# Two attention layers on one core: v's weights loaded twice, and another order for loads, combinations and the first layer 1 projections

## Chip, core and metric

The kernel runs on one core of one Trainium2 chip. The metric is the device time of one execution in microseconds (us). The median of three runs of the kernel before is 4241.31 us (4237.41 to 4242.2). Engines are called PE (matrix multiply), DVE (vector), ACT (scalar and activation functions), POOL and SP; SP only issues transfers here, and ACT and POOL can issue them too.

## What is computed

The input x is 8 images of 512 channels and 1024 tokens (32 x 32). All is float32. In short:

```python
def gn(v):                      # per image and group of 16 channels (G=32)
    return (v - mean) / sqrt(var + eps)

def layer0(x):                  # 8 heads of 64 channels
    n = gn(x) * gn_w + gn_b
    q, k, v = split(qkv_w @ n + qkv_b)
    a = softmax((q*s)^T (k*s)) @ v
    return proj_w @ (x + a) + proj_b

def layer1(x):
    q, k, v = w_q @ x, w_k @ x, w_v @ x
    attn = einsum('gh,bhqT->bgqT', w_head, q^T k * scale)   # heads are mixed
    attn = softmax(attn)
    attn = (attn - mean) / sqrt(var + eps) * gamma + beta   # per image and head
    return w_proj @ rearranged(attn @ v) + b_proj

x = x + layer0(gn(x))
x = x + layer1(gn(x))
```

## The kernel before

One program runs everything. Batches (images) are taken one after the other: layer 0 for all eight, with its result kept in DRAM (`x1_d`), then layer 1 for all eight. Within each engine the instructions run in the order in which the Python code issues them, apart from a short setup of constants ahead of that. Work that must be slipped between other work is put into an `Agenda`: `ag.at(slot, fn)` stores a function, and `ag.run(slot)` calls what is stored for that slot, in the order in which it was stored.

**Projections.** A projection of 512 x 512 weights with a 512 x 1024 right side is done with seven half-size products instead of eight. The weights' side needs seven tiles: three are blocks loaded as they are, four are sums and differences. `load_blocks(which)` (lines 747 to 763) issues eight DMAs of 128 KB; `combine_left(which)` (lines 765 to 776) makes the four combinations on DVE (parts 0 to 3) and stores all seven tiles to DRAM (part 4, on SP), from where `load_left` fetches them in later batches. The tag `left` has two buffers, so a third set waits until the first is free. The right side's combinations are `combine_right` (lines 882 to 885). `project0` runs the seven products on PE: products 1 and 2, then 6, 5, 7, 3 and 4, with ACT or DVE taking each out of PSUM (the addition of product 6 is line 932, that of product 7 line 939). Products 1 and 4 use the two PSUM buffers `a0`, products 5 to 7 the two double tiles `s`.

**Start of the kernel.** SP issues the four loads of x for batch 0. `load_blocks("k", nc.scalar)` and the same for v issue theirs from ACT. POOL loads the small vectors, qkv's bias among them and, last, `whT`. DVE copies the bias into `bq`, takes x's statistics (`bn_stats`, line 648), and with a small matmul (`pm`, line 622) the group means follow. A tiny matmul `pw` (line 555) belongs to the setup. Then come, in the code's order: `combine_right`, `combine_left("k")`, `qk0(0,"k")`, `combine_left("v")`, `load_blocks("q")`, `combine_left("q")`, `v0(0)`, `load_blocks("p")`, `combine_left("p")`, `qk0(0,"q")`, and attention of batch 0.

**Seam.** In the last batch of layer 0, `first_k1`, `first_q1` and `first_v1` project k, q and half of v of layer 1's batch 0. q's copy is written in another order of elements, with strided views (line 1019). The final totals of the attention (matmul `z`, line 1128, in an `a0` buffer) fall between the two projections. `out0` follows.

**Layer 1.** A batch has NX = 32 half steps, numbered x, and some after them. Half step x does the scores of x (line 1656, PE), copies them to a tile `raw` (ACT and DVE), and does for older steps: mixing of heads (`mix` of y = x - 4, line 1706), exponentials, sums and squares, and `values` (line 1752). Two half steps make one t. Before mixing, the tile `raw` of t is regrouped by eight DMAs of 256 KB each (`regroup`, line 1682, index r) into one half of `re_t`; t takes the half (t + b) % 2. In the first half steps (x up to 4) all eight are issued at once; later they are tied one by one to matmuls.

v is made in four pairs of 128-token blocks (`v_pair`, line 1475): pairs 0 and 1 between the steps that close the batch before, pairs 2 and 3 among the first scores. v's weights (`load_w`, line 1339, four DMAs of 256 KB) lie in that half of `re_t` which t = 1 will fill, in its first four r. So pairs 2 and 3 must be done before the regroups r = 0 to 3 of t = 1 may be issued: the code gives t = 1 its own order, and puts pair 3 into slot 3 - 0.75, which half step 3 runs ahead of its regroups. In batch 0 the group statistics of batch 7 (`group_stages`: means, squares, root) and `v_sums` fall here too. A PSUM tile of the tag `m` (three buffers) is held until its last reader has been issued and is done; scores, mixes, pairs and the small matmuls of the statistics all use this tag.

The sums of exponentials are kept in a tile `z` (tag `z`, one buffer, 1 MB) and their squares in `z2`; a quarter of the batch (`qb`) uses them from its first `squares` to its `totals`.

Between two batches the order is: k's projection of the next batch among the last half steps, pair 0, the division and the affine step, the output projection `out1` with its loads `xs` and the load of left_q, pair 1, q's projection.

Of the kernel before, what the change touches and what calls it, by code (L numbers as in the profile page):

```python
# [9 lines left out]
F32 = mybir.dt.float32  # L10
# [8 lines left out]
P = 128  # L19
# [448 lines left out]
def tile_two_attention_layers(  # L468
# [19 lines left out]
    nc = tc.nc  # L488
    B, C, T = x_d.shape
    H = w_head.shape[0]  # L490
    D = C // H
    NCC = C // P
# [28 lines left out]
    qkvb = column("qkvb", qkv_b)  # L521
# [175 lines left out]
    with ExitStack() as l0:  # L697
# [49 lines left out]
        def load_blocks(which, queue=nc.sync, tag="u0"):  # L747

            t = left_tile(which, 0)
            if tag == "junk":  # L750
                a21[which] = zpool.tile([P, T], F32, tag=tag, name=f"a21_{which}", bufs=1)[
                    :, :C
                ].rearrange("p (k o) -> p k o", k=2)
            else:
                a21[which] = zpool.tile([P, 2, HC], F32, tag=tag, name=f"a21_{which}")
            for dst, i, j in (
                (t[:, 0], 0, 0), (t[:, 1], 0, 1), (a21[which], 1, 0), (t[:, 2], 1, 1),
            ):
                for k in range(2):
                    queue.dma_start(  # L760
                        out=dst[:, k],
                        in_=SOURCES[which][ts(2 * j + k, P), i * HC : (i + 1) * HC],
                    )
# [11 lines left out]
            if 4 in parts:  # L775
                nc.sync.dma_start(out=left_d[which], in_=t.rearrange("p f k o -> p (f k o)"))

        load_blocks("k", nc.scalar)
        load_blocks("v", nc.scalar)


        bq = wpool.tile([P, 3, NCC], F32, tag="bq", name="bq", bufs=1)
        nc.vector.tensor_copy(bq.rearrange("p i c -> p (i c)"), qkvb)

        st0 = {}
        n_t, xa_t, q_t, k_t, v_t = {}, {}, {}, {}, {}
# [404 lines left out]
        qk0(0, "k")  # L1191
        combine_left("v")
        load_blocks("q")
        combine_left("q")
        v0(0)
        load_blocks("p")
        combine_left("p")
        qk0(0, "q")
        tmp.clear()

        for b in range(B):
            more = b + 1 < B
            ag = Agenda()
            ag.at(1, lambda: bias_xa(b))
            for c in range(NCC):
                ag.at(2 + 2 * c, lambda c=c: start_xa(b, c))
            for c, slot in enumerate((4, 7, 12, 15)):
                if b > 0:
                    ag.at(slot, lambda c=c: stats_out(b - 1, c))
                if more:  # L1210
                    ag.at(slot + 1, lambda c=c: load_x(b + 1, c))
            if b < 3:

                which = ("k1", "q1", "p1")[b]
                ag.at(1, lambda which=which: load_blocks(which, tag="junk"))
                for i, slot in enumerate((13, 14, 16, 17, 19)):
                    ag.at(slot, lambda which=which, i=i: combine_left(which, [i]))
            if more:
                stats0(b + 1, ag, 20)
                for c in range(NCC):  # L1220
                    ag.at(49 + 4 * c, lambda c=c: normalize0(b + 1, c))
                ag.at(32, lambda: load_left("k", b + 1))
                ag.at(33, lambda: load_left("v", b + 1))
            else:

                def load_first():
                    t = n_t["1"] = shared.tile([P, NCC, T], F32, tag="n", name="y_0")
                    for c in range(NCC):
                        nc.sync.dma_start(out=t[:, c], in_=x1_d[0][ts(c, P), :])

                ag.at(20, load_first)
                for slot, fn in zip((22, 25, 28), group_stages(0, B - 1, small_psum)):
                    ag.at(slot, fn)
                ag.at(32, lambda: load_left("k1", 0))
                ag.at(33, lambda: load_left("q1", 0))
                for c in range(NCC):
                    ag.at(49 + 4 * c, lambda c=c: normalize_to(n_t["1"][:, c], 0, c))
            attention0(b, ag)
            slot = NI + 2
            if more:  # L1240
                combine_right(f"{b + 1}", n_t[b + 1])
                qk0(b + 1, "k")
            else:
                combine_right("y1", n_t["1"])
                first_k1()
            ag.flush()
            if more:
                load_left("q", b + 1)
                v0(b + 1)
                load_left("p", b)  # L1250
                qk0(b + 1, "q")
            else:
                load_left("p", b)
                first_q1()
                first_wv()
            combine_right(f"{b}_xa", xa_t[b])
            out0(b)
            tmp.clear()
# [6 lines left out]
    with ExitStack() as l1:  # L1265
# [373 lines left out]
        class Attention1:  # L1639
# [5 lines left out]
            def scores(self, x, i):  # L1645

                b, t, hp = self.b, x // 2, x % 2 * 2 + i
                qb, kb = t // NKB, t % NKB
                nm = f"s1_{b}_{x}_{i}"
                ps = m_psum(nm)  # L1650
                pv = ps.rearrange("p m (j k) -> p m j k", j=2)
                for j in range(2):
                    for c in range(2):
                        for m in range(2):
                            r = slice(m * D, m * D + D)
                            last = nc.tensor.matmul(  # L1656
                                pv[c * D : c * D + D, m, j],
                                qo_t[b][r, 2 * qb + j, hp, ts(c, D)],
                                k_t[b][r, hp, ts(kb, KB)], start=True, stop=True,
                            )  # L1660
                if x > MLAG:
                    self.piece(last)
                if x % 2 and i == 1:

                    order = (4, 5, 6, 7, 0, 1, 2, 3) if t == 1 else R_ORDER
                    self.due = [(t, r) for r in order]
                if x % 2 == 0 and i == 0:
                    self.raw[t] = rawpool.tile([P, H, 2, KB], F32, tag="raw", name=f"raw_{b}_{t}")
                dst = self.raw[t][:, 2 * hp : 2 * hp + 2]
                if i == (x == 0) and (x < MLAG or x % 2):  # L1670
                    nc.vector.tensor_copy(dst, pv)  # L1671
                else:
                    nc.scalar.copy(dst, pv)  # L1673
# [205 lines left out]
            def half_step(self, x, ag):  # L1879
                y, w = x - MLAG, x - MLAG - 1  # L1880
                if 0 <= w < NX:
                    self.squares(w, 0)
                    self.sum_e(w, 0)
                if x < NX:
                    self.scores(x, 0)
                if 0 <= w < NX:
                    self.squares(w, 1)
                    self.sum_e(w, 1)
                if x < NX + MLAG:
                    k_leave()  # L1890
                if 0 <= w < NX:
                    self.sum_e2(w, 0)
                    self.sum_e2(w, 1)
                k_leave()
                if 0 <= y < NX:
                    self.mix(y, 0)
                if 0 <= w < NX:
                    self.values(w, 0)
                if x < NX:
                    self.scores(x, 1)  # L1900
                if 0 <= y < NX:
                    self.mix(y, 1)
                ag.run(x - 0.75)
                if x <= MLAG or x >= NX:
                    self.regroup(n=NR)
                if x >= NX:
                    self.piece(n=len(self.pieces))
                ag.run(x - 0.5)
                if 0 <= w < NX:
                    self.values(w, 1)  # L1910
                    self.e.pop(w)
                    if w % QLAG == QLAG - 1:
                        qb = w // QLAG
                        self.leave(qb)
                        self.totals(qb)
                        if qb < NQB - 1:
                            ag.at(x + 2, lambda: self.reciprocals(qb, ag, x + 2))
                            ag.at(x + 6, lambda: self.divide(qb))
                ag.run(x)


        load_w(("v", 0), wvT, re_t[:, 1, : NCC * C])

        NV = NT // 4
        for b in range(B):
            more = b + 1 < B
            a = Attention1(b)
            ag = Agenda()

            for i, slot in enumerate((1, 3 - 0.75)):  # L1930
                ag.at(slot, lambda i=i: v_pair(b, NV + i))
            if b == 0:
                for x, fn in enumerate(group_stages(B - 1, B, small_psum1)):
                    ag.at(x, fn)
                ag.at(3 - 0.75, v_sums)
            free = (NX // 2 - 2 + b) % 2
            if more:
                a.pieces += [lambda i=i: y_piece(b + 1, i) for i in range(4 * NCC)]
# [43 lines left out]
            op = out1(b, right_o)  # L1982
            load_left(("q", b + 1))
            v_pair(b + 1, 1)
            op.run()
            q_projection(b + 1).run()

# [69 lines left out]
```

## Time and profile before

| | |
|---|---|
| median of three runs | 4241.31 us |
| the profiled execution's own time | 4225.8 us |
| its span, first to last instruction | 4223.7 us |
| first k matmul of layer 0 | 24.16 us |
| first scores of layer 0 | 104.38 us |
| first scores of layer 1, batch 0 | 1813.03 us |
| first mix of layer 1, batch 0 | 1847.57 us |
| a group of first scores in batches 1 to 7 of layer 1 | 2132.39, 2439.50, 2745.39, 3052.20, 3357.86, 3662.68, 3967.83 us |
| DMA, all queues | 521.99 MB, mean 124 GB/s |

The page shows one profiled execution. Groups of instructions are named by line, engine, operation and tiles; a timeline row gives start, duration, engine, line, operation, what is written and read, and in brackets how long the engine had stood before and who released it. "issue" in the place of a releaser means that the engine waited for nothing that the profile shows. The profiled execution is 15.5 us shorter than the median of the timed runs; its parts are compared with each other and with those of another profiled execution.

The costliest groups of each engine, for scale (idle time of the engine ahead of them after the bar):

```profile
L1706 PE MATMUL m<-wmix,re 64*64 64x64 f32 x32768 | 591.2, 219 | 17.3 <-issue 12.0
L1752 PE MATMUL a<-e,v 128*64 128x256 f32 x4096 | 556.3, 392 | 2.6 <-ACT z L1723 1.7
L1656 PE MATMUL s<-k,q 64*64 64x256 f32 x8192 | 553.7, 388 | 5.6 <-DVE q L1512 2.6
```

### The profile page before, as it was taken

How to read it: one execution, taken by the hardware profiler on the slowest of the kernel's cores; microseconds unless marked ns; L12 is line 12 of the kernel's file. 1: busy time of each engine (PE TensorE's matmuls, PEld its weight loads, DVE VectorE, ACT ScalarE, POOL GpSimd, SP SyncE). 2: the span in 40 equal slices, each digit the busy share in tenths (PEclk: the TensorE clock that was granted, in tenths of full speed). 3: DMA queues.
4: the chain of work that ended last, by engine and by line, in shares of the span. 5: the costliest groups of instructions: out<-in, count | busy, mean ns of one | idle time of the engine just before them, and what ended most of it. 6: DMA issues, size and time to landing. Idle time of an engine off the chain costs nothing.

```text
span 4223.7 us, 131372 instructions
## 1 busy us (share of the span) xinstructions
PE 4147.2 (98%) x58572; PEld 2212.8 (52%) x58572; DVE 2861.1 (68%) x3780; ACT 2317.5 (55%) x2735; POOL 60.3 (1%) x86
## 2 busy tenths in 40 slices
PE   7999999999999999999999999999999999999998
PEld 4353535353535353356556466466466466466565
DVE  4748484747475757558758668668578578588587
ACT  1717272726263635358358368278287187286386
POOL 0000000000000000000000000000000000000000
PEclk9999999999999999999999999999999999999999
DMA  4213131212121212167467367277287386385475
GB/s 150 79 45 114 46 111 48 84 48 84 46 86 43 87 45 86 43 156 196 141 149 194 125 172 193 104 192 186 104 204 188 95 205 168 112 207 150 135 183 141
DMA packets 253871, 521.99 MB, mean 124 GB/s; under 512 B 51888, under 2 KB 59440, under 8 KB 246640
## 3 DMA queue, kind: packets, MB, share of 16 engines
q1 hardware_dynamic: 248416, 510.71, 42.6%
q8 instruction: 461, 7.55, 0.7%
q0 software_dynamic: 2576, 0.69, 0.4%
q10 hardware_dynamic: 2304, 2.10, 0.2%
q14 instruction: 114, 0.93, 0.1%
HBM read 197.16 MB, written 46.92 MB: 58 GB/s over the span
## 4 chain that ended last, share of the span: by engine, by line
PE 92%; DVE 4%; DMA 2%; ACT 1%; issue 1%; SPq 0%; POOL 0%; DVEq 0%; ACTq 0%; POOLq 0%
PE a L1752 12%; PE s L1656 11%; PE m L1706 11%; PE s L1083 11%; PE a L1109 10%; PE pp_p L903 5%; PE pk_p L903 5%; PE pq_p L903 4%; PE pv_p L903 4%; PE pk L1400 4%; PE pq L1400 4%; PE pv L1475 4%; PE pp L1400 3%; PE t L1783 1%; DMA re<-raw 1%
## 5 line engine op out<-in xcount | busy, mean ns | idle before, releaser
L1706 PEld LDWEIGHTS m<-wmix,re 64*64 64x64 f32 x32768 | 580.5, 135 | 113.3 <-issue 49.1
L1088 ACT ACTIVATE e<-s 128x1024 f32<-128x1024 f32 x512 | 497.2, 1026 | 233.6 <-PE s L1083 232.6
L1706 PE MATMUL m<-wmix,re 64*64 64x64 f32 x32768 | 591.2, 219 | 17.3 <-issue 12.0
L1712 ACT ACTIVATE e<-m 128x1024 f32<-128x1024 f32 x512 | 526.2, 1028 | 135.7 <-PE m L1706 132.1
L1730 DVE TENSOR_TENSOR z<-z,e 128x1024 f32<-128x1024 f32 x448 | 537.9, 1220 | 72.2 <-ACT e L1712 72.0
L1734 DVE TENSOR_TENSOR z<-z,e 128x1024 f32<-128x1024 f32 x448 | 534.7, 1221 | 61.9 <-ACT e L1723 60.8
L1656 PE MATMUL s<-k,q 64*64 64x256 f32 x8192 | 553.7, 388 | 5.6 <-DVE q L1512 2.6
L1752 PE MATMUL a<-e,v 128*64 128x256 f32 x4096 | 556.3, 392 | 2.6 <-ACT z L1723 1.7
L1096 DVE TENSOR_TENSOR zacc<-zacc,e 128x1024 f32<-128x1024 f32 x384 | 468.8, 1221 | 87.0 <-ACT e L1088 65.9
L1673 ACT COPY raw<-s 128x1024 f32<-128x1024 f32 x368 | 372.9, 1013 | 269.2 <-PE s L1656 232.0
L1083 PE MATMUL s<-q,k 64*64 64x512 f32 x4096 | 490.1, 593 | 2.3 <-ACT e L1088 2.3
L1109 PE MATMUL a<-e,v 64*64 64x512 f32 x4096 | 484.0, 589 | 0.0
L1723 ACT ACTIVATE e<-e 128x1024 f32<-128x1024 f32 x448 | 460.2, 1057 | 0.0
L1656 PEld LDWEIGHTS s<-k,q 64*64 64x64 f32 x8192 | 269.0, 132 | 269.2 <-issue 164.4
L1752 PEld LDWEIGHTS a<-e,v 128*64 128x64 f32 x4096 | 250.5, 136 | 123.6 <-issue 13.0
L1109 PEld LDWEIGHTS a<-e,v 64*64 64x64 f32 x4096 | 156.6, 133 | 282.9 <-issue 282.9
L1083 PEld LDWEIGHTS s<-q,k 64*64 64x64 f32 x4096 | 147.8, 133 | 275.3 <-issue 241.4
L1671 DVE COPY raw<-s 128x1024 f32<-128x1024 f32 x144 | 176.0, 1222 | 91.1 <-PE s L1656 84.8
L1475 PE MATMUL pv<-re,y 128*128 128x512 f32 x480 | 214.8, 601 | 0.0
L1475 PEld LDWEIGHTS pv<-re,y 128*128 128x128 f32 x480 | 89.3, 191 | 113.5 <-issue 112.7
L903 PE MATMUL pv_p<-left_v,tmp 128*128 128x256 f32 x512 | 114.9, 383 | 4.2 <-DVE tmp L932 4.2
L1480 DVE COPY v<-pv 128x512 f32<-128x512 f32 x30 | 20.7, 690 | 138.4 <-ACT v L1479 138.4
(315 smaller groups left out, 4051.5 us busy)
## 6 DMA issues: line engine op xcount, KB each, us to landing
re<-raw SPq DMA_DIRECT2D x1024, 256.0 KB
rzb<-zd SPq DMA_DIRECT2D x256, 128.0 KB
left_q<-left_q SPq DMA_DIRECT2D x17, 1792.0 KB
left_p<-left_p SPq DMA_DIRECT2D x17, 1792.0 KB
left_k<-left_k SPq DMA_DIRECT2D x10, 1792.0 KB
x<-in_x_dram SPq DMA_DIRECT2D x32, 512.0 KB
x<-x SPq DMA_DIRECT2D x64, 256.0 KB
left_v<-left_v SPq DMA_DIRECT2D x8, 1792.0 KB
```

The costliest lines, as they stand in the source:

```text
L903: nc.tensor.matmul(out, st, mv, start=start, stop=(k == 1), skip_group_check=True)
L1083: nc.tensor.matmul(ps[c * D : c * D + D, m], k[r, hp, k0 : k0 + D], q[r, hp, ts(f, FB)], start=True, stop=True,)
L1088: nc.scalar.activation(e[i], ps, AF.Exp, scale=S0 * S0)
L1096: nc.vector.tensor_add(zacc[g], zacc[g], e[i])
L1109: nc.tensor.matmul(acc[g][a][m * D : m * D + D], v[rows, kc, ts(2 * hp + m, D)], e[i][rows, m], start=(kc == 0), stop=(kc == NG - 1),)
L1475: nc.tensor.matmul(ps[:, m], y_t[b][:, c, ts(2 * i + m, P)], w[:, c], start=(c == 0), stop=(c == NCC - 1),)
L1656: last = nc.tensor.matmul(pv[c * D : c * D + D, m, j], qo_t[b][r, 2 * qb + j, hp, ts(c, D)], k_t[b][r, hp, ts(kb, KB)], start=True, stop=True,
L1706: last = nc.tensor.matmul(ps[c * D : c * D + D, a, ts(r, D)], self.re[t, r][rows, j, k0 : k0 + D], wmix[rows].rearrange("p g i -> p (g i)" ...
L1712: nc.scalar.activation(self.e[y][:, j], ps.rearrange("p a c -> p (a c)"), AF.Exp)
L1730: nc.vector.tensor_add(self.z[:, j], self.z[:, j], self.e[y][:, j])
L1734: nc.vector.tensor_add(self.z2[:, j], self.z2[:, j], self.e2[j])
L1752: last = nc.tensor.matmul(self.acc[w][two * D : two * D + D, s].rearrange("p (c i) -> p c i", i=Q8), v_t[b][:, kc, ts(g, D)], e[:, g], sta ...
```

## The change

The diff does these things:

1. `load_blocks("k")` and `load_blocks("v")` are issued from SP, in the code's order behind x's four loads. `bq` is a view of `qkvb` instead of a copy.
2. `combine_left("q")` moves behind `v0(0)`, its store behind `qk0(0,"q")`; `combine_left("p")` moves behind `qk0(0,"q")` and q's store.
3. `first_q1` comes before `first_k1`, and their loads change places too.
4. In layer 1, a new function `load_wv_again(b)` loads v's weights into a tile of the tag `z`. It is called ahead of batch 0, in place of the load into `re_t`, and for each later batch after pair 1, so that pairs 2 and 3 (and `v_sums`) read that tile. The load into `re_t` near the end of each batch stays for pairs 0 and 1.
5. t = 1 is regrouped in the same order as every t. Pair 3 and `v_sums` move from slot 3 - 0.75 to slot 3, the call for slots x - 0.75 is gone, and the group statistics' three stages are put into slots 0, 1 and 3 ahead of the pairs (before: 0, 1 and 2, behind the pair in slot 1).

```diff
-        load_blocks("k", nc.scalar)
-        load_blocks("v", nc.scalar)
-
-
-        bq = wpool.tile([P, 3, NCC], F32, tag="bq", name="bq", bufs=1)
-        nc.vector.tensor_copy(bq.rearrange("p i c -> p (i c)"), qkvb)
+        load_blocks("k")
+        load_blocks("v")
+
+
+        bq = qkvb.rearrange("p (i c) -> p i c", i=3)
...
         load_blocks("q")
-        combine_left("q")
         v0(0)
+        combine_left("q", range(4))
         load_blocks("p")
+        qk0(0, "q")
+        combine_left("q", [4])
         combine_left("p")
-        qk0(0, "q")
         tmp.clear()
...
-                ag.at(32, lambda: load_left("k1", 0))
-                ag.at(33, lambda: load_left("q1", 0))
+                ag.at(32, lambda: load_left("q1", 0))
+                ag.at(33, lambda: load_left("k1", 0))
...
                 combine_right("y1", n_t["1"])
-                first_k1()
+                first_q1()
...
                 load_left("p", b)
-                first_q1()
+                first_k1()
                 first_wv()
...
                 if x % 2 and i == 1:
-
-                    order = (4, 5, 6, 7, 0, 1, 2, 3) if t == 1 else R_ORDER
-                    self.due = [(t, r) for r in order]
+                    self.due = [(t, r) for r in R_ORDER]
...
-                ag.run(x - 0.75)
                 if x <= MLAG or x >= NX:
                     self.regroup(n=NR)
...
-        load_w(("v", 0), wvT, re_t[:, 1, : NCC * C])
+        def load_wv_again(b):
+
+            t = zpool.tile([P, 2, T], F32, tag="z", name=f"wv_{b}")
+            load_w(("v", b), wvT, t.rearrange("p j c -> p (j c)"))
+
+        load_wv_again(0)
...
-            for i, slot in enumerate((1, 3 - 0.75)):
-                ag.at(slot, lambda i=i: v_pair(b, NV + i))
             if b == 0:
-                for x, fn in enumerate(group_stages(B - 1, B, small_psum1)):
+                for x, fn in zip((0, 1, 3), group_stages(B - 1, B, small_psum1)):
                     ag.at(x, fn)
-                ag.at(3 - 0.75, v_sums)
+            for i in range(NV):
+                ag.at(1 + 2 * i, lambda i=i: v_pair(b, NV + i))
+            if b == 0:
+                ag.at(3, v_sums)
...
             v_pair(b + 1, 1)
+            load_wv_again(b + 1)
             op.run()
```

## The prediction

> **What bounds the kernel now.** I read the page first: busy table, slices, chain by line. Then the gaps on PE in order of time through the timeline, then the timeline of all engines around each gap that the diff touches.
>
> ```profile
> PE 4147.2 (98%) x58572; PEld 2212.8 (52%) x58572; DVE 2861.1 (68%) x3780; ACT 2317.5 (55%) x2735; POOL 60.3 (1%) x86
> ...
> PE 92%; DVE 4%; DMA 2%; ACT 1%; issue 1%; SPq 0%; POOL 0%; DVEq 0%; ACTq 0%; POOLq 0%
> ```
>
> PE is busy for 4147.2 of 4223.7 us and holds 92% of the chain. No matmul is added or removed, so all that the change can win or lose is the 76.5 us in which PE stands. The Trainium skill (Perfetto Trace Analysis, "Identifying the Most-Contended Engine") says that matmul busy time is no measure of the distance to the roofline; I use it only to find the gaps. The list of PE's waits over the whole span names those that matter:
>
> ```profile
> PE pw L555 <- DVE eye L551: 17.4, 1, 17.4
> PE m L1706 <- issue: 12.0, 22, 1.4
> ...
> PE pv_p L903 <- DVE tmp L932: 4.2, 1, 4.2
> PE pk_p L903 <- DVE n L861: 4.2, 1, 4.2
> ```
>
> The columns are: who waited for whom, us in total, times, longest. The first and fourth are the start of the kernel, the third is the first v projection, the second is spread over layer 1. The seam between the layers adds rows of 1 to 3 us. Each is taken below.
>
> **The change, part by part.** Everything is summed against the profiled execution (span 4223.7, its own time 4225.8), and the gain is then taken off the median.
>
> **Part 1, start.** k's and v's blocks go from ACT's queue to SP's, behind the four x loads; the copy into bq is gone.
>
> ```profile
> 10.80 0.17 DVE L783 COPY bq<-qkvb 128x12 f32<-128x12 f32 x1 [9.58 <-DMA qkvb<-in_qkv_b_dram]
> ...
> 18.56 0.16 DVE L626 COPY gs_gm<-pm 128x4 f32<-128x4 f32 x1 [0.28 <-PE pm L622]
> ...
> 24.16 8.53 PE L903 MATMUL pk_p<-n,left_k 128*128 128x512 f32 x16 [4.19 <-DVE n L861]
> ```
>
> DVE is in order and stands until 10.80 for the bias of qkv, with the statistics of x queued behind. They then run without a gap for 5.7 us, the last tile's from 15.11. In the packets of the DMA queues x's last one lands near 14.2 us, because k's and v's 2.1 MB share the engines: the skill (DMA: Bandwidth & Descriptors, "Issuing engines are not separate DMA queues", and "Queues, rings and completion order") says that queues issued by different engines run on the same 16 DMA engines, which serve them in turn. The trace agrees: while SP's and ACT's queues are both full the engines move 180 to 390 GB/s for both together. So dropping the copy alone is worth at most 15.11 - 14.2 = 0.9 us. With x alone in front, 2.1 MB at the 333 to 394 GB/s of the stretch from 3 to 6 us, and a start at 1.8, are in by 8 to 9 us, the last statistics end near 10.2 instead of 16.6. What is late next: PE's tiny matmul pw (line 555) stands ahead of the statistics' pm in PE's queue and needs whT, a POOL DMA issued at 6.56 that takes 7.1 us to land, 13.7 us. Then pw 0.59, pm and the copy gs_gm near 14.85 instead of 18.56: 3.7 us. If pm is ordered ahead of pw, or whT lands earlier, up to 16.6 - 10.2 = 6.4. I take 4.0, range 0.9 to 6.4. The k blocks issue from about 6.5 us on SP and are in by 14, before n is ready near 20; v's by 17, needed near 46. Nothing on SP waits behind them but left_k's store, issued at 32.1.
>
> **Part 2, combinations.** q's go behind v0, p's behind q's projection.
>
> ```profile
> 64.47 0.69 DVE L768 TENSOR_TENSOR left_q<-a_q,left_q 128x512 f32<-128x512 f32 x1 [11.30 <-DMA left_q<-in_qkv_wT_dram]
> ...
> 67.01 1.21 DVE L932 TENSOR_TENSOR tmp<-tmp,pv_p 128x1024 f32<-128x1024 f32 x1
> ...
> 68.28 5.23 PE L903 MATMUL pv_p<-left_v,tmp 128*128 128x256 f32 x16 [4.21 <-DVE tmp L932]
> ```
>
> DVE's queue holds q's four combinations ahead of v0's addition at line 932. They wait until 64.47 for q's blocks, which came behind left_v's store; the addition, ready near 60.5 (its product is the first half of PE's 7.07 us from 57.00), runs at 67.01 and PE stands 4.21 us for the PSUM tile that it frees. With the combinations behind v0 the addition runs at once: -4.2, and I find nothing that takes its place. The combinations (4 x 0.69 = 2.7 us) then run while PE does the first 16 matmuls of q (7.0 us), which read only loaded blocks. q's store (SP) now stands behind p's eight issues (3.6 us) and nobody waits for it soon. p's combinations run on DVE after q's last additions, 2.7 us ahead of nb and the first zacc; ACT's first use of nb came at 109.60, 4.3 us after it was made at 105.34, so they fit; without that cover they would cost at most 2.7. I take 0.
>
> **Part 3, q1 before k1.** q1's strided additions take 2.05 us a pair (line 1019), k1's 1.28 (line 1002). PE's 1.72 us stand before out0 is the time until the last of q1's are out of PSUM. Now it falls after q1, where the totals' matmul z (0.57) and its row copy use the same two PSUM tiles: PE resumes about 2.8 us after q1's end, against 0.8 now between k1's end and q1's start; after k1 out0 starts with no stand. Net +0.2, range -0.3 to +1.
>
> **Part 4, start of layer 1, batch 0.** The squares of the group statistics go ahead of the v pair, the root from slot 2 to slot 3.
>
> ```profile
> 1830.52 0.36 PE L633 MATMUL pv<-gs_sq,gavg 128*128 128x4 f32 x2 [2.15 <-DVE gs_sq L631]
> ...
> 1833.25 1.96 PE L1656 MATMUL s<-k,q 64*64 64x256 f32 x32 [0.48 <-DVE raw L1671]
> ```
>
> PE's 2.15 and 0.48 us stands come from a chain of four small DVE operations behind the v pair's copies. Ahead of the pair the chain (four steps of 0.2) starts when raw's copy ends, 1820.06, so PE stands 0.9. But its PSUM tile is then held until slot 3, so the scores of x = 2 and 3 share two tiles of three: I count 0.5 + 0.2 + 0.4 of new stands. 2.63 - 2.0 = -0.6, range -1.8 to +1.5. The first pair's weights, loaded to another tile, arrive before 1820 either way.
>
> **Part 5, the second load of v's weights and the regroups of t = 1.** This is the part that repeats, seven times.
>
> ```profile
> 2442.55 19.15 SPq L1682 DMA_DIRECT2D re<-raw  x16
> ...
> 2464.38 0.27 PE L1706 MATMUL m<-wmix,re 64*64 64x64 f32 x2 [1.43 <-issue]
> ```
>
> Half of t = 1's regroups write where v's weights lie, and wait for the batch's last v pair (7.13 us from 2452.08) to end, 2459.2; the 1 MB then lands by 2464.7, under the first mixes, which issue most instructions per us. At that place PE stands in batches 1 to 7 for 0.76, 1.43, 1.34, 0.76, 1.66, 0.47 and 0.34 us: 6.8 us together. What stands there reads t = 0's rows, landed by 2452, so it isn't their data. I take it for instruction fetch: the skill (Advanced Engine Details and Errata, "ISA Cache") gives blocks of 16 KB, 256 instructions; queue 8's 461 packets of 7.55 MB are such blocks, and one moved in the us from 2461. The stands end as the regroups' packets end. With the weights in the sums' tile all eight regroups go from 2453 and, at t = 0's 8.7 us for 2 MB, end near 2462.5, 2.2 us earlier than now; that clears most. I take -5.0, range 0 to -7. Batch 0 has no stand there, so nothing.
>
> What it adds: four DMAs of 256 KB on SP per batch, after left_q's and before the output's stores. SP waits for nothing there (the sums' tile was last read by the totals at 2067, the issue comes near 2078). The loads end near 2091 where left_q's packets ended at 2088.2; the first pair that reads them starts at 2134, and the tile's first sum comes after both pairs. x's and left_q's transfers are ahead of them in the queue. Cost 0; upper end +2 in all.
>
> **Sum.** -4.0 - 4.2 + 0.2 - 0.6 - 5.0 = -13.6: the profiled execution to 4212.2. The median shown, 4241.3, lies 15.5 above the profiled execution; I take the same gain off it: 4227.7.
>
> **The rivals.** First, the issue stands stay (the block's fetch meets the regroups anyway, since they still run until 2462.5 and PE stood from 2462.95): only 8.6 are won, 4232.7. For it: the DMA engines are 76 to 87% busy from 2453 to 2465, and the same bytes move. Against: the stands end with the last packets. Chance 0.24.
>
> Second, the start gives all 6.4 and the other parts their best (6.4 + 4.2 + 0.3 + 1.8 + 6.8 = 19.5): 4221.8. For it: pw has no part in the statistics. Against: the order of the two on PE today. Chance 0.13.
>
> Third, slower: the 7 extra MB collide with left_q. x's residual, left_q and v's weights are 5.0 MB from 2075.6; q's projection starts at 2105.9. Should the engines serve all at once, they need over 164 GB/s; below it each lacking us counts seven times, and at 149 GB/s it is 3.2 x 7 = 22 us, which puts the time at 4241.3 - 13.6 + 22 = 4250. From 2078 to 2090 the trace shows 265 to 341 GB/s, and left_q is issued first, so: 0.05.
>
> **How the numbers follow.** Forecast 0.58, own range 4223 to 4232. What a measurement of this kernel can tell from no change is about 0.2%, 8.5 us. The forecast is nearly always faster by more; of the first rival half is faster and half within; the second is faster. Faster 0.79, within 0.16, slower 0.05. Range 4219 to 4238: from the second rival less the runs' spread of 3 to the first plus the worst of parts 3, 4 and 5's loads (0.8 + 2.1 + 2.0).
>
> **What would show it.** Right: the first k matmul near 20; no stand at v0's third product; the eight regroups of t = 1 in one run before the last pair ends, and PE's stands 25 us into each batch gone. Wrong: a first k matmul at 23 or later; PE waiting for left_p, left_q or z; issue stands of the old size; a start of layer 1 longer than 33 us from its first scores to the first mix.

## Result, and the profile after

| | before | after |
|---|---|---|
| median of 11 timed runs each | 4238.94 us | 4230.70 us |
| lowest to highest | 4233.37 to 4242.20 | 4225.78 to 4238.67 |
| the profiled execution's own time | 4225.8 us | 4230.7 us |
| its span | 4223.7 us | 4228.9 us |

The ratio after to before is 0.9981, with a 95% interval of 0.9973 to 0.9990: 8.1 us won (4.2 to 11.4), where 13.6 were forecast. The two profiled executions say the opposite, 5.2 us longer. The profiled execution of before, 4225.8 us, lies below all eleven timed runs of that kernel. So the spans alone are not compared here; timed runs are, and single stages of the traces.

The page of the kernel after, its busy table, and the list of PE's waits (who waited for whom; us in total, times, longest):

```profile
PE 4152.5 (98%) x58572; PEld 2215.3 (52%) x58572; DVE 2861.2 (68%) x3779; ACT 2319.1 (55%) x2735; POOL 60.3 (1%) x86
```

```profile
PE m L1704 <- issue: 17.7, 24, 2.5
...
PE pk_p L902 <- DVE n L860: 4.2, 1, 4.2
...
PE pm L622 <- DVE gs_m L620: 2.8, 2, 2.4
...
PE s L1656 <- issue: 2.2, 1, 2.2
PE z L1127 <- DVE q L1018: 1.7, 1, 1.7
...
PE pv L633 <- DVE gs_sq L631: 1.5, 2, 0.8
```

PE executes the same 58572 matmuls. The wait of the first v projection (pv_p for tmp, 4.2) has left the list; the wait for n at the start is as long as before; the first row, mixes that wait for nothing the profile shows, grew from 12.0 to 17.7.

**Layer 0.** The timeline around the start and around q's first projection (start, duration, engine and line, operation, what is written and read; in brackets the stand ahead of it and its releaser):

```profile
11.40 1.29 DVE L648 BATCH_NORM_STATS2 bn<-x 128x6 f32<-128x512 f32 x2 [0.73 <-DMA x<-in_x_dram]
14.14 0.56 PE L555 MATMUL pw<-whT,eye 8*128 8x8 f32 x2 [14.14 <-DVE blk L565]
15.26 0.16 DVE L626 COPY gs_gm<-pm 128x4 f32<-128x4 f32 x1 [0.28 <-PE pm L622]
20.83 9.74 PE L902 MATMUL pk_p<-n,left_k 128*128 128x512 f32 x16 [4.17 <-DVE n L860]
...
58.60 1.22 DVE L931 TENSOR_TENSOR tmp<-tmp,pv_p 128x1024 f32<-128x1024 f32 x1 [7.54 <-PE pv_p L902]
68.69 3.62 PE L902 MATMUL pv_p<-left_v,tmp 128*128 128x256 f32 x16
72.95 0.68 DVE L768 TENSOR_TENSOR left_q<-a_q,left_q 128x512 f32<-128x512 f32 x1
```

The last statistics of x start at 11.40 us instead of 15.11, and what is late next is pw, as forecast (whT's transfer landed at 14.00; blk, which the bracket names, isn't read by pw): pm and its copy end at 15.4, and k's first matmul starts at 20.83 instead of 24.16. v0's addition (line 931) now runs at once at 58.60, and q's combinations come behind it at 72.95, under q's own matmuls. The start of each stage, by its first PE row in the two timelines:

| start of | before | after | difference |
|---|---|---|---|
| k, batch 0 of layer 0 | 24.16 | 20.83 | -3.33 |
| v | 49.99 | 47.86 | -2.13 |
| q | 80.25 | 72.14 | -8.11 |
| second group of first scores | 106.61 | 98.50 | -8.11 |
| first scores of layer 1 | 1813.03 | 1805.41 | -7.62 |
| first mix of layer 1 | 1847.57 | 1840.77 | -6.80 |
| scores of layer 1, batch 2 | 2439.50 | 2433.45 | -6.05 |
| scores of layer 1, batch 4 | 3052.20 | 3050.73 | -1.47 |
| scores of layer 1, batch 7 | 3967.83 | 3970.76 | +2.93 |

The 8.1 us are there when q starts, and keep until layer 1. From there to batch 7 this pair of executions loses 10.6 us (-7.62 to +2.93). Part of that is at the place where part 5 should have won, for example in batch 2:

```profile
2436.51 16.88 SPq L1680 DMA_DIRECT2D re<-raw  x16
...
2446.03 7.13 PE L1475 MATMUL pv<-wv,y 128*128 128x512 f32 x16
...
2455.81 1.09 PE L1704 MATMUL m<-wmix,re 64*64 64x64 f32 x59
2459.35 0.28 PE L1704 MATMUL m<-wmix,re 64*64 64x64 f32 x3 [2.45 <-issue]
...
2460.72 2.13 PE L1704 MATMUL m<-wmix,re 64*64 64x64 f32 x64
```

The order is what the change says: the row of 16 regroups (t = 0's and t = 1's) runs through to 2453.4, as the batch's last v pair ends at 2453.2. PE still stands, 2.45 us ahead of the mix at 2459.35, where before it stood 1.43 us at 2464.38. And the next 64 mixes take 2.13 us, where 64 mixes of the same shape take 1.11 us a little later: from 2459.81 to 2463.23 the granted clock of PE is 0.50.

### The profile page after: what moved, and what is told of

It reads as the page before. It is cut to its first block, busy times and chain, and to the rows that moved or that the text cites. A ratio compares the mean times of both kernels' runs of the same rounds, so it can differ in the third digit from the quotient of the medians.

```text
span 4228.9 us, 131405 instructions
## 1 busy us (share of the span) xinstructions
PE 4152.5 (98%) x58572; PEld 2215.3 (52%) x58572; DVE 2861.2 (68%) x3779; ACT 2319.1 (55%) x2735; POOL 60.3 (1%) x86
## 4 chain that ended last, share of the span: by engine, by line
PE 92%; DVE 3%; DMA 2%; ACT 1%; issue 1%; SPq 0%; DVEq 0%; ACTq 0%
PE a L1750 12%; PE m L1704 11%; PE s L1656 11%; PE s L1082 10%; PE a L1108 10%; PE pv_p L902 5%; PE pp_p L902 5%; PE pk_p L902 5%; PE pq_p L902 4%; PE pk L1400 4%; PE pq L1400 4%; PE pv L1475 4%; PE pp L1400 3%; DMA re<-raw 1%; PE t L1781 1%
## 5 line engine op out<-in xcount | busy, mean ns | idle before, releaser
L1704 PE MATMUL m<-wmix,re 64*64 64x64 f32 x32768 | 592.2, 219 | 24.5 <-issue 17.7
L1475 PE MATMUL pv<-wv,y 128*128 128x512 f32 x256 | 116.3, 608 | 0.3 <-DVE raw L1669 0.3
L902 PE MATMUL pq_p<-tmp,left_q 128*128 128x512 f32 x256 | 112.5, 592 | 0.0
```

Source lines behind the costliest of these rows:

```text
L902: nc.tensor.matmul(out, st, mv, start=start, stop=(k == 1), skip_group_check=True)
L1704: last = nc.tensor.matmul(ps[c * D : c * D + D, a, ts(r, D)], self.re[t, r][rows, j, k0 : k0 + D], wmix[rows].rearrange("p g i -> p (g i)" ...
```

## Where part 5's gain went: the packets

The packet records of the transfers tell more than the rows. Queue 8 carries blocks of 16 KB; the prediction took them for PE's instructions, and the counts fit: 58572 matmuls and as many weight loads in 461 blocks are 254 to a block. In the table, all times are us after the start of the batch's group of scores: the start of the block's packet that comes in the mixes' first dense stretch, the end of the last packet of the regroups of t = 1, and PE's stand there (batches 1 to 7; stands under 0.2 us are given as 0). "left out" is an experiment below in which the regroups of t = 1 aren't issued.

```
batch                            1      2      3      4      5      6      7
before      block's packet   23.33  22.49  24.08  22.13  24.60  22.34  24.82
            regroups end     25.2 to 26.2
            stand             0.76   1.43   1.34   0.76   1.66   0.47   0.34   sum 6.8
after       block's packet   23.31  23.18  23.49  23.39  23.50  23.30  23.28
            regroups end     23.53  24.87  23.48  23.81  23.54  23.49  23.42
            stand             1.21   2.45   1.11   2.24   0.91   1.50   0.00   sum 9.4
left out    block's packet   22.26  20.79  22.45  21.22  22.96  21.78  23.19
            stand             0.00   0.00   0.00   0.00   0.00   0.00   0.00   sum 0
pairs_late  block's packet   21.93  20.87  22.08  21.06  23.20  21.35  22.50
            regroups end     21.0 to 22.2
            stand             0.00   0.30   0.00   0.00   0.75   0.00   0.00   sum 1.05
```

Without the transfers the block's packet starts between 20.8 and 23.2 us. In the kernel after it starts in every batch as the burst ends, with at most 12 of the 2048 data packets of the 16 regroups still to start (in batch 2 two of them start only as the block's packet ends, hence the 24.87). The difference, after less left out, is 1.05, 2.39, 1.04, 2.17, 0.54, 1.52 and 0.09 us, and PE's stands are within 0.4 of that: 1.21, 2.45, 1.11, 2.24, 0.91, 1.50 and 0. PE goes on about 1.4 us (1.3 to 1.6) after the packet has ended: in batch 2 the packet lasts from 2456.63 to 2457.90 and PE resumes at 2459.35; in before, 2461.99 to 2462.94 and 2464.38. In the kernel before the block started 0.4 to 3.2 us ahead of the end of the regroups, with 18 to 278 of the 2048 packets still to start: late, but in most batches not held until the end. So the burst ends about 2 us earlier, as forecast, and the block comes no earlier. That the block is held until the burst is nearly over is what happened, not a rule: in layer1_part below, with the same layer 1, batch 2's block starts at 22.41 with 115 data packets still to start, 1.6 us later than without the transfers, and the stand is 1.64. What fits all of these cases is that the stand is as long as the block's delay. The profile puts before's stand of 1.66 in batch 5 down to ACT; it too ends 1.4 us after its block's packet, and is counted here.

## The experiments

In what was expected, theory A is the one formed from these traces: the whole gain is layer 0's (parts 1 and 2), and part 5 gives nothing because PE's stands are instruction blocks held up by the regroups' burst, which the change moves and doesn't remove. The rivals are named in each expectation. Each ratio is to runs of before on the same chip.

**layer0_part: the kernel before with parts 1 and 2 alone.**

```diff
-        load_blocks("k", nc.scalar)
-        load_blocks("v", nc.scalar)
+        load_blocks("k")
+        load_blocks("v")
-        bq = wpool.tile([P, 3, NCC], F32, tag="bq", name="bq", bufs=1)
-        nc.vector.tensor_copy(bq.rearrange("p i c -> p (i c)"), qkvb)
+        bq = qkvb.rearrange("p (i c) -> p i c", i=3)
-        combine_left("q")
         v0(0)
+        combine_left("q", range(4))
         load_blocks("p")
-        combine_left("p")
         qk0(0, "q")
+        combine_left("q", [4])
+        combine_left("p")
```

> The kernel before with parts 1 and 2 alone (loads of k and v from SP, bq as a view, combinations behind v0 and behind q's projection). Theory A (all of the gain is made in layer 0, layer 1 gives nothing): the second group of layer 0's first scores at 98.5 us instead of 106.6, and the time 8 us under the kernel before, ratio 0.9981. Theory B (the prediction's part 5 holds and the profile after was an unlucky one): about 8 of 13 us, and the layer 1 part alone is worth 5.

Measured: median 4234.60 us in 17 runs against 4244.03; ratio 0.9976 (0.9968 to 0.9983), that is 10.2 us (7.2 to 13.6). The second group of first scores starts at 97.13. PE's stands 25 us into the batches add up to 7.05, as in before. This half of the diff alone gives at least what the whole diff gives.

**layer1_part: the kernel after with layer 0's start of before.** The diff is the one above, undone in the changed kernel.

```diff
-        load_blocks("k")
-        load_blocks("v")
+        load_blocks("k", nc.scalar)
+        load_blocks("v", nc.scalar)
...
-        combine_left("q", range(4))
+        combine_left("q")
```

> The kernel before with parts 3, 4 and 5 alone (q1 before k1, second load of v's weights, regroups of t = 1 in one run, other slots). Theory A: ratio 1.000 within 0.001, and PE's stands about 25 us into batches 1 to 7 add up to more than the 6.8 us of before (the profile after has 9.4). Theory B: 5 us under the kernel before, ratio 0.9988, and those stands add up to under 3 us.

Measured: 4244.71 against 4244.03; ratio 0.9999 (0.9991 to 1.0007): -0.4 us (-3.8 to +3.0). Its list of PE's waits has the first v projection's stand back, and stands by issue of the size of the kernel after:

```profile
PE m L1704 <- issue: 17.7, 28, 1.7
...
PE pv_p L903 <- DVE tmp L932: 4.2, 1, 4.2
```

At part 5's place they add up to 8.8 us. Parts 3, 4 and 5 together are worth nothing that can be measured. The 4.2 of the second row isn't its whole price, as the account of part 2 below shows.

**t1_left_out: the kernel after without the regroups of t = 1 in batches 1 to 7**, so that their mixes of t = 1 read older rows.

```diff
                     self.re[t, r] = ...
+                    if t == 1 and self.b > 0:
+                        continue
                     dma = nc.sync.dma_start(out=self.re[t, r], in_=self.raw[t][r::NR])
```

> The changed kernel without the eight regroups of t = 1 in batches 1 to 7 (the mixes of t = 1 read older rows, so the output of these batches differs); every PE instruction stays where it was. Theory A (the fetch of PE's next block waits for these packets): the stands 25 us into batches 1 to 7 fall from 9.4 us to under 1.5. Theory B (pairs_late lost the stands because PE's order changed): they stay at 8 to 9 us.

Measured: 4224.52 us in one run, and in the timeline of batch 2:

```profile
2437.52 6.38 SPq L1682 DMA_DIRECT2D re<-raw  x8
...
2455.03 1.11 PE L1706 MATMUL m<-wmix,re 64*64 64x64 f32 x64
...
2456.82 1.12 PE L1706 MATMUL m<-wmix,re 64*64 64x64 f32 x64
```

PE's work is the same, in the same order, and the row of 59 mixes, a stand and 3 mixes has become a row of 64. So in all seven batches: the stand is gone. This is what ties the stands to the transfers. The list of all its waits still has 15.9 us by issue at line 1706, at other places of layer 1, which this study doesn't explain.

**pairs_late: the v pairs of batches 1 to 7 both in slot 3.** The regroups of t = 1 then go before both pairs, 14 us of PE's work ahead of the mixes.

```diff
-                ag.at(1 + 2 * i, lambda i=i: v_pair(b, NV + i))
+                ag.at(1 + 2 * i if b == 0 else 3, lambda i=i: v_pair(b, NV + i))
```

> The changed kernel with both v pairs of batches 1 to 7 in slot 3, behind the first four half steps' scores, so that the regroups of t = 0 and t = 1 start some 7 us earlier against the first mix; nothing else. Theory A (PE stands because the fetch of its next instruction block waits for the regroups' packets): their packets end ahead of the first mix, and the stands 25 us into batches 1 to 7 fall from 9.4 us to under 2; time 5 to 9 us under the changed kernel, ratio to before 0.996 to 0.997. Theory B (the stands belong to the mix itself, or to the fetch whatever the traffic is): stands stay near 9 us and the time is that of the changed kernel, 0.998.

Measured: 4223.57 us (5 runs) against 4244.03; ratio 0.9952 (0.9938 to 0.9966), 20.4 us under before. It was forecast at 0.996 to 0.997 and gave somewhat more. Batch 2 in its timeline:

```profile
2435.02 12.73 SPq L1680 DMA_DIRECT2D re<-raw  x16
2437.31 14.00 PE L1475 MATMUL pv<-wv,y 128*128 128x512 f32 x32
...
2453.95 1.09 PE L1704 MATMUL m<-wmix,re 64*64 64x64 f32 x59
2455.34 0.28 PE L1704 MATMUL m<-wmix,re 64*64 64x64 f32 x3 [0.30 <-issue]
```

The row of regroups ends 15.8 us after the start of the batch's group of scores (2431.97) instead of 19.9, the packets end at about the time at which the block comes without them, and the same stand is 0.30 instead of 2.45. Over the batches 9.4 became 1.05. The ratios of the two kernels to before lie 0.0029 apart, 12.3 us, and the stands at this place explain 8.4 of them. Most of the rest is at hand in the record of the granted clock: in the kernel after it falls to 0.50 from 2459.81 to 2463.23 and from 3077.63 to 3081.04, just behind the two longest stands (2.45 and 2.24 us, batches 2 and 4), and in pairs_late it stays at 1.00 from 1842 to 4214. At half speed 3.41 us do 1.7 us of work, so I estimate up to 3.4 us for the two. This edit is possible because of the second load of v's weights: with them in `re_t`, pair 3 must end before half of the regroups.

**t1_in_halves: the kernel after, with the second half of t = 1's regroups behind pair 3 again**, as before, but with the weights in the new tile.

```diff
-                    self.due = [(t, r) for r in R_ORDER]
+                    order = (4, 5, 6, 7, 0, 1, 2, 3) if t == 1 else R_ORDER
+                    self.due = [(t, r) for r in order]
...
-                    self.regroup(n=NR)
+                    self.regroup(n=NR // 2 if x == 3 else NR)
...
-                ag.at(1 + 2 * i, lambda i=i: v_pair(b, NV + i))
+                ag.at(1 + 2 * i, lambda i=i: v_pair(b, NV + i) if i == 0
+                      else a.regroup(v_pair(b, NV + i), NR // 2))
```

> The changed kernel, but of the regroups of t = 1 r = 0 to 3 are tied behind the last matmul of the batch's last v pair, as the old place of the weights made them; the weights stay in the sums' tile, PE's order is that of the changed kernel. Theory A (the one run of eight is what lengthens the stands): the stands 25 us into batches 1 to 7 come back to those of the kernel before, 6.8 to 7.4 us in all, with 1.4 and 0.8 us in batches 2 and 4 instead of 2.4 and 2.2. Theory B (the second load or the slots lengthen them): they stay at 9.3 us.

Measured: 4234.49 us in one run. The stands are 1.22, 0.91, 1.26, 0.61, 1.83, 1.42 and 0.89, sum 8.1. In batches 2 and 4, where the kernel after lost most (2.45 and 2.24), they fell to the size of before; in batches 6 and 7 they did not. The second half ended at 26.5 to 27.2 us here and at 25.2 to 26.2 in before, so the kernels differ in more than the split, and the sum lies between the two that were set against each other. That a split burst lets the block through earlier is supported in two batches and not settled as a rule.

**warm_start: twelve small matmuls ahead of k's first**, into a PSUM tile nobody reads.

```diff
         first.flush()
+        wt = score_psum("warm")
+        for i in range(12):
+            nc.tensor.matmul(wt[:, 0, :P], ones, gavg, start=True, stop=True)
         for c in range(NCC):
             normalize0(0, c)
```

> The changed kernel with 12 small matmuls of constants into an unused PSUM tile between the statistics' last matmul and k's projection, nothing else. Theory A (PE starts k's projection at half clock after standing 4.2 us, and this eats 1.2 us of the 3.3 won at the start): k's first 16 matmuls take 7 us instead of 9.7, v's projection starts near 45 us instead of 47.9. Theory B (the slow start is not the clock): v's projection starts at 47.9 or later.

Measured: 4226.52 us in one run. Its timeline:

```profile
16.38 4.52 PE L1188 MATMUL warm<-gavg,ones 128*128 128x128 f32 x24
20.73 7.11 PE L902 MATMUL pk_p<-n,left_k 128*128 128x512 f32 x16
```

k starts 0.1 us earlier than in the kernel after and its first 16 matmuls take 7.11 instead of 9.74; v starts at 45.13 instead of 47.86, 2.7 earlier. So PE's 4.2 us of standing at this place cost about 2.6 us more in the matmuls behind it (less in some other executions, as part 1 below shows).

**means_behind: in batch 0 of layer 1 the first v pair goes ahead of the means of the group statistics.**

```diff
             if b == 0:
+                ag.at(0, lambda: v_pair(0, NV))
                 for x, fn in zip((0, 1, 3), group_stages(B - 1, B, small_psum1)):
                     ag.at(x, fn)
-            for i in range(NV):
+            for i in range(b == 0, NV):
```

> The changed kernel with the third v pair of layer 1's batch 0 in slot 0, ahead of the group means; nothing else. Theory A (PE stands 2.4 and 0.7 us for the small chain and then runs the pair at half clock, 9.3 instead of 7.1 us): both stands and the slow pair go, and the first mix comes 30 to 31.5 us after batch 0's first scores, against 35.4 in the changed kernel and 34.5 before. Theory B (the wait for the copies of the pair takes the place): 34 us or more.

Measured: 4230.15 us in one run. From the first scores (1804.59) to the first mix (1836.37) it takes 31.78 us, where after took 35.36 (1805.41 to 1840.77) and before 34.54. Its timeline:

```profile
1806.48 7.13 PE L1475 MATMUL pv<-wv,y 128*128 128x512 f32 x16
1815.18 0.36 PE L622 MATMUL pm<-gs_m,gavg 128*128 128x4 f32 x2 [1.57 <-DVE gs_m L620]
...
1818.66 0.36 PE L633 MATMUL pv<-gs_sq,gavg 128*128 128x4 f32 x2 [1.23 <-DVE gs_sq L631]
```

The pair is back at 7.13 us. The stand for the means shrank from 2.36 to 1.57 only, and the one for the squares grew from 0.66 to 1.23, so 3.6 us were won, a little less than hoped for. Against three traces in which the old order ran its pair at full clock (33.3 to 33.6 us for the stage, see part 4 below), 1.5 to 1.8 are left.

**bias_view: the kernel before with bq as a view, and nothing else.**

```diff
-        bq = wpool.tile([P, 3, NCC], F32, tag="bq", name="bq", bufs=1)
-        nc.vector.tensor_copy(bq.rearrange("p i c -> p (i c)"), qkvb)
+        bq = qkvb.rearrange("p (i c) -> p i c", i=3)
```

> The kernel before with the bias as a view and nothing else. The prediction's term: worth at most 0.9 us, so k's first matmul at 23.3 to 24.2 us instead of 24.16. Rival (the copy, not the transfers, held up the statistics): k's first matmul near 21.

Measured: 4238.62 us in one run; k's first matmul starts at 23.80, 0.36 earlier than in before.

```profile
13.04 1.29 DVE L648 BATCH_NORM_STATS2 bn<-x 128x6 f32<-128x512 f32 x2 [4.85 <-DMA x<-in_x_dram]
```

With the bias out of the way DVE stands for x instead, whose third tile it gets only at 13.04, while k's and v's blocks are in transfer too. The wait named in the profile of before was the bias, and it hid this one; moving the blocks in addition brings k's start to 20.37 (layer0_part). Moving the blocks without the view was not tried.

**all_three: pairs_late, warm_start and means_behind together.**

```diff
+                ag.at(0, lambda: v_pair(0, NV))
...
-            for i in range(NV):
-                ag.at(1 + 2 * i, lambda i=i: v_pair(b, NV + i))
+            for i in range(b == 0, NV):
+                ag.at(1 + 2 * i if b == 0 else 3, lambda i=i: v_pair(b, NV + i))
```

> pairs_late, warm_start and means_behind together on the changed kernel. If the three are independent: 12 us (pairs_late against the changed kernel) plus 2.7 plus 3 to 5 under the changed kernel's 0.9981, that is a ratio to before of 0.9935 to 0.9945. If the fetches' stands elsewhere in layer 1 grow in exchange: 0.995 or more.

Measured: 4210.07 us (6 runs) against 4240.00; ratio 0.9935 (0.9921 to 0.9950), 27.6 us under before, at the better end of what was expected of three independent gains. It is faster than both kernels.

## Why the prediction was right and wrong

The direction and the range held. The size was 8.1 instead of 13.6, and the time is that of the first rival, 8.6 won and the issue stands staying. The parts in layer 0 gave what was forecast or more (8.2 forecast for parts 1 and 2, 10.2 measured in layer0_part), the parts in layer 1 gave nothing (5.4 forecast for parts 3 to 5, -0.4 measured in layer1_part). The range held because it reached to the first rival, not because its largest single part came true.

One premise failed in several parts: "all that the change can win or lose is the 76.5 us in which PE stands". The same matmuls take longer behind a stand, so PE's busy time moves too (4147.2 before, 4152.5 after). By the prediction's own parts:

**Part 1, start: -4.0 forecast, -3.3 at k's start, -2.1 by v's.** The copy alone is worth 0.36 (the bound was 0.9), whT's landing and pw come next (14.14 against 13.7), gs_gm at 15.26 against 14.85. One step of the chain was off: the statistics end at 12.93, not near 10.2, since DVE still stood 1.71 and 0.73 us for x's last two tiles (2.1 MB at 333 to 394 GB/s from 1.8 us on are in by 7 to 8 us, the prediction wrote 8 to 9, and the last tile came near 11.4). It cost nothing, because pw couldn't start before 14.1 either way.

Between k's start and v's another 1.2 us went, and that isn't the change's doing. PE stands 4.2 us for n in both kernels, and k's 16 first matmuls then take 8.53 us in before and 9.74 in after; but with before's start they take 9.73 in bias_view and 8.85 in layer1_part, and with after's 8.84 in layer0_part and 8.68 in t1_in_halves. Over all traces without the warm matmuls v starts at 49.99 to 50.98 with the old start (three traces) and at 45.83 to 47.99 with the new one (six), so the pair of profiles shows nearly the least of the gain. The length follows the clock: the first entry in the trace's record of it, full speed, comes at 27.00 us in before, 26.11 in after and 23.84 in layer0_part, that is 2.84, 5.28 and 3.47 us after k's start, and half of these is what the 16 matmuls took above the 7.11 of warm_start, where the entry comes at 19.73, ahead of k. The Trainium skill (TensorE: Matmul & The Clock Gate, "What's actually happening") says that the array runs at half clock after an idle window of about 3.4 us; the durations agree, with matmuls of 0.85 us in the first 5 us of k's and of 0.43 after. Yet the stands of 2.45 and 2.24 us in layer 1, shorter than that window, were followed by half clock too. Ahead of that first entry the profile prints 1.00 for the clock. At a later place it shows it (start and end, then busy times and counts; the last three are granted clock, DMA share and GB/s):

```profile
20.80:25.00 4.20, 4.17 (x5) 1.85 (x6) 4.10 (x4) 1.89 (x3) 0.00 (x0) 1.00 0.00 0
...
1813.60:1818.00 4.40, 4.40 (x6) 1.88 (x7) 0.00 (x0) 0.03 (x1) 0.00 (x0) 0.50 0.70 178
```

Five matmuls in 4.17 us with a clock of 1.00 written beside them: at the start of a kernel the durations are to be believed.

**Part 2, combinations: -4.2 forecast, -6.0 measured.** v took 30.26 us (49.99 to 80.25) and takes 24.28 (47.86 to 72.14). The stand of 4.21 is gone, as forecast, and p's combinations cost nothing. Mis-sized was the stand's price: the row behind it, quoted in the prediction, shows 16 matmuls in 5.23 us, where the row at 68.69 above takes 3.62 (in before the granted clock is 0.50 from 67.96 to 71.37). Those 1.6 us could have been read off before.

**Part 3, q1 before k1: +0.2 forecast, nothing measured.** PE's stand went over from out0 to z and k1, as said, but with 1.73 and 0.36 instead of 1.72 and 0.21; out0 starts with none. Together with the rest of the seam the stage is within 0.1 of before.

**Part 4, start of layer 1: -0.6 forecast, +0.8 in this pair of traces.** The stand for the squares is 0.66, less than the 0.9 counted. But the small matmuls now stand in front of the pair, and PE reaches it after stands of 1.40, 2.36 and 0.66 us:

```profile
1809.72 0.39 PE L622 MATMUL pm<-gs_m,gavg 128*128 128x4 f32 x2 [2.36 <-DVE gs_m L620]
1810.04 2.53 PE L1656 MATMUL s<-k,q 64*64 64x256 f32 x32
1813.23 0.56 PE L633 MATMUL pv<-gs_sq,gavg 128*128 128x4 f32 x2 [0.66 <-DVE gs_sq L631]
1813.65 9.32 PE L1475 MATMUL pv<-wv,y 128*128 128x512 f32 x16
```

The pair takes 9.32 us at a granted clock of 0.50 in its first half (the row of windows above), against 7.13 in means_behind and 8.26 in before. But this too changes from one execution to the next. Six traces have layer 1's start as in the kernel after: in three of them (after, layer1_part, t1_left_out) the pair takes 9.3 us and the stage from first scores to first mix 35.36; in the other three (pairs_late, warm_start, t1_in_halves), with the same code there, the stage takes 33.3 to 33.6. With before's code it takes 34.1 to 34.8 in three traces. So these traces don't tell whether part 4 wins or loses: the 1.8 to 2.0 us between its two groups are more than the part. All are inside its range. The prediction's sign of being wrong for this stage, longer than 33 us, didn't fit its own sum: 34.54 less 0.6 is 33.9.

**Part 5: -5.0 forecast, 0 measured.** Here a step fails, and it was the largest term of the sum. "The stands end as the regroups' packets end", and with their end moved 2.2 us earlier "that clears most". The first half was an observation from before; the runs put another in its place. PE goes on when its instruction block has arrived, about 1.4 us after that block's packet. t1_left_out shows that the transfers are what delays the block. In the kernel before the block got in ahead of the last regroups; in the kernel after it starts as the burst ends, in all seven batches. So an earlier end of the burst doesn't help while the burst still covers the time at which the block comes without it, 20.8 to 23.2 us into the batch; pairs_late moves the end to 21.0 to 22.2, and the stands go. The burst's new end itself, 23.4 to 23.8 us after the scores in six batches, or 2462.9 to 2463.3 on before's scale, was forecast well (2462.5, though the 2453 and 8.7 that it was made of give 2461.7). That no more than 0 came of it is measured over timed runs (layer1_part, -3.8 to +3.0). That the stands grew is seen in more than one pair of traces: 6.8, 7.05 and 7.35 us with before's layer 1 (before, layer0_part, bias_view), 9.4, 8.8, 9.25 and 8.3 with after's (after, layer1_part, means_behind, warm_start). The added 7 MB of loads show no cost anywhere that I found.

What stays open: which of layer 1's other stands by issue come and go between executions (12.0 to 23.0 us at the mixes' line in these profiles), and with them why one profile of after is longer than one of before while eleven runs of each say the contrary; why the block waits at times until the burst is nearly over and at times not; and whether one queued burst holds up a block longer than two shorter ones (t1_in_halves).

## What to carry to other kernels

A stand of PE can cost more than its length, by the half-clock matmuls behind it (1.6 us behind 4.2 here): compare the row behind the gap with a row of the same shape elsewhere, and count the difference into the sum. How much it is can change from one execution to the next (8.5 to 9.8 us for k's first 16 matmuls), so look at more than one trace. When PE waits for nothing that the profile shows, look at which transfers run at that moment and at the packets of the instruction queue: here a bulk transfer just ahead of a stretch of many short instructions had to end by the time at which that stretch's block comes without it, and ending it 2 us earlier, but still too late, gave nothing. Where single executions differ by as much as the change is worth, compare stages of the traces, and leave the sum to timed runs.

## What the hardware showed that I had not expected

- An instruction block's packet of 16 KB came up to 2.4 us later behind eight queued regroups (2 MB) than without them, and PE resumed about 1.4 us after the packet's end.
- The granted clock falls to 0.50 for 3.41 us, in some places for twice that (6.83). In the kernel after it did so behind single stands of 2.45 and 2.24 us.
- The same code with nearly the same stands ran slow in one execution and not in the next: after stands of 1.40, 2.36 and 0.66 us within 9 us, the third v pair of layer 1's batch 0 took 9.32 us in the kernel after; in pairs_late, after 1.40, 2.36 and 1.23, it took 7.11.
- 12 small matmuls (4.5 us of PE) ahead of k's projection made its first 16 matmuls 2.6 us shorter, for nothing but being there.
